# One shape of TensorE tile, 64 rows by 32 columns, for the attention to the context

## The chip, the cores and the metric

The kernel runs on one core of one Trainium2 chip. The core has a matrix engine (TensorE, called PE in the profile, with its weight loads as PEld), three engines for vectors (VectorE or DVE, ScalarE or ACT, GpSimd or POOL) and a queue for transfers (SyncE or SP). They run side by side and wait for each other through semaphores. The metric is the device time of one execution in microseconds, as a median of runs.

## The reference

It is one transformer block in 32-bit floats on x of 2 x 1024 x 256, with a context of 2 x 154 x 192: self-attention, attention to the context, and a gated feed-forward layer, each behind a layer norm and added to x. There are 16 heads of 64.

```python
def _attention(xq, xkv, wq, wk, wv, wo, bo):
    q = (xq @ wq).reshape(B, S, N_HEADS, D_HEAD)
    k = (xkv @ wk).reshape(B, T, N_HEADS, D_HEAD)
    v = (xkv @ wv).reshape(B, T, N_HEADS, D_HEAD)
    attn = jnp.einsum('bihd,bjhd->bhij', q, k) * scale
    attn = jax.nn.softmax(attn, axis=-1)
    out = jnp.einsum('bhij,bjhd->bihd', attn, v).reshape(B, S, D_ATTN)
    return out @ wo + bo

x = _attention(_layernorm(x), _layernorm(x), sa_...) + x
x = _attention(_layernorm(x), cond, ca_...) + x
p = _layernorm(x) @ ff_w1 + ff_b1
x = (p[:, :DF] * gelu(p[:, DF:])) @ ff_w2 + ff_b2 + x
```

## The kernel before

The array of TensorE, 128 rows by 128 columns, can be divided into tiles. A matmul uses the rows on whose partitions its operands lie and the columns on whose partitions its result lies: with 64 rows of operands and 32 partitions of result there are eight such tiles, with 64 by 64 four, with 64 by 128 two, with 128 by 128 one. [...]

The work goes in units: a unit is one sequence (of two) and one pair of heads (of eight), so sixteen units in each attention. A pair of heads fills 128 partitions, 64 each. The order of all instructions is written out by hand: one loop runs over the slots of self-attention, one over the 48 slots c of the attention to the context (three for each unit), one over the slots of the feed-forward layer. Each slot emits its pieces one after another, and each engine executes its own in that order.

In self-attention everything is in tiles of 64 by 32, apart from the values' projection: the projections of queries and keys (`project_both`, L352, with m = KB = 32), the scores (`scores`, L483) and the weighed values (`weigh`, L530).

A slot of the attention to the context holds these pieces:

- `cross_first` (L772) computes the scores of three tiles of 128 queries (two in every third slot), both heads, against the 154 keys of the context. Each matmul takes 64 rows (the head's dimension), 128 queries as its columns, and 154 keys as its moving operand. VectorE takes the maximum of each row, ScalarE the exponent, and a slot later VectorE and GpSimd divide by the sum.
- `cross_queries` (L352) projects the queries of the next unit, in every slot n = 0. Without an argument it uses m = P = 128 columns. Only the first unit's, which is emitted during self-attention through `cross_pieces`, is called with KB.
- `cross_drain` transposes the weights on VectorE, and `cross_regroup` moves them with eight transfers, so that two blocks of 32 keys lie together on 64 partitions.
- `cross_weigh` calls `cross_values` (L851) twice, which multiplies the weights by the values: 64 rows (keys), 64 columns (one head's dimension), 256 queries as the moving operand, three groups m of keys summed up in PSUM.
- Between them stand the output projections (L457), the values' projection of the context (L733), the keys of the context (L717), and the transposes of the layer norm (L270), which all take the whole array.

At the beginning of this stage the last pieces of self-attention (L530) are interleaved with its slots, at its end the first of the feed-forward layer (`gate_slot`, L933). The results of matmuls go to three pairs of PSUM banks: ps_s for scores and gates, ps_m and ps_o for the rest. A bank is used again when its reader has copied it out.

## Time and profile before

| | |
|---|---|
| time, median of 3 runs | 1115.72 us (1113.64 to 1117.36) |
| the profiled execution's own time | 1111.62 us |
| its span, from the first to the last instruction | 1109.7 us |
| instructions | 44860 |
| granted clock of TensorE | 1.00 |
| self-attention, with its preparation | up to about 722 us, the first scores of the context at 709.9 |
| attention to the context | from there to about 940 us |
| feed-forward layer | 918 us to the end |
| busy time of the scores, L772, in all | 41.6 us, 512 records |
| projected queries, L352, in 64 by 128 | 54.1 us, 240 records |
| weighed values, L851 | 35.2 us and 20.6 us, 768 records |

A line of a group or of the timeline names the line of the kernel, the operation, what it writes and reads, and for TensorE the tile of the array ("64*32") ahead of the moving operand ("64x512"). A matmul in 32-bit floats shows as two records, each with its weight load. Ends of matmuls are modelled, so the starts of what follows say more than durations. Busy time of a group is the time in which at least one of its records runs. In a table by stage each engine has its busy microseconds and, in brackets, its count.

### The profile page before, as it was taken

How to read it: one execution, taken by the hardware profiler on the slowest of the kernel's cores; microseconds unless marked ns; L12 is line 12 of the kernel's file. 1: busy time of each engine (PE TensorE's matmuls, PEld its weight loads, DVE VectorE, ACT ScalarE, POOL GpSimd, SP SyncE). 2: the span in 40 equal slices, each digit the busy share in tenths (PEclk: the TensorE clock that was granted, in tenths of full speed). 3: DMA queues.
4: the chain of work that ended last, by engine and by line, in shares of the span. 5: the costliest groups of instructions: out<-in, count | busy, mean ns of one | idle time of the engine just before them, and what ended most of it. 6: DMA issues, size and time to landing. Idle time of an engine off the chain costs nothing.

```text
span 1109.7 us, 44860 instructions
## 1 busy us (share of the span) xinstructions
PE 1093.7 (99%) x18436; PEld 733.5 (66%) x18436; DVE 855.1 (77%) x1205; ACT 628.2 (57%) x2030; POOL 681.4 (61%) x1584
## 2 busy tenths in 40 slices
PE   8999999999999999999999999999999999999998
PEld 6555656546556566666566565576766777888887
DVE  5889999898999899999999999868777875322222
ACT  4766666766666666667667666655556553121111
POOL 2777877777877787777777777756656653220000
PEclk9999999999999999999999999999999999999999
DMA  3222212111111012011111111136665443000000
GB/s 83 67 59 57 56 28 52 43 41 42 25 40 42 23 42 47 13 43 42 23 42 33 32 33 28 38 87 158 167 164 126 113 107 77 10 11 10 20 10 19
DMA packets 102350, 59.66 MB, mean 54 GB/s; under 512 B 31994, under 2 KB 92930, under 8 KB 102146
## 3 DMA queue, kind: packets, MB, share of 16 engines
q1 hardware_dynamic: 100914, 56.15, 21.3%
q8 instruction: 145, 2.38, 0.9%
q10 hardware_dynamic: 1232, 0.66, 0.2%
q14 instruction: 59, 0.48, 0.1%
HBM read 27.12 MB, written 2.10 MB: 26 GB/s over the span
## 4 chain that ended last, share of the span: by engine, by line
PE 56%; ACT 11%; DVE 10%; POOL 8%; DMA 7%; issue 4%; SPq 4%; DVEq 0%; POOLq 0%; ACTq 0%
PE pa L933 10%; ACT p L494 10%; PE po L530 8%; PE s L483 8%; DVE st L645 6%; DMA st<-st 6%; PE py_ca L457 5%; PE pf L956 5%; PE pq_ca L352 4%; PE poc L851 4%; SPq L504 3%; POOL p L595 3%; PE sc L772 3%; PE py_sa L457 2%; PE pk_sa L352 2%
## 5 line engine op out<-in xcount | busy, mean ns | idle before, releaser
L494 ACT ACTIVATE p<-s,st 128x512 f32<-128x512 f32 x512 | 344.9, 686 | 194.0 <-DVE st L645 186.0
L595 POOL TENSOR_SCALAR p<-p,rd,ee 128x512 f32<-128x512 f32 x512 | 385.7, 768 | 46.7 <-DVE rd L591 45.4
L645 DVE TENSOR_REDUCE st<-s 128x2 f32<-128x1024 f32 x256 | 300.9, 1216 | 20.3 <-PE s L483 7.1
L609 DVE STREAM_TRANSPOSE pT<-p 128x1024 f32<-128x1024 f32 x256 | 302.3, 1218 | 0.3 <-POOL p L595 0.3
L483 PE MATMUL s<-k_sa,q_sa 64*32 64x512 f32 x4096 | 262.1, 592 | 7.4 <-ACT p L494 6.5
L530 PE MATMUL po<-pT,v_sa 64*32 64x256 f32 x8192 | 239.5, 376 | 0.9 <-DVE pT L609 0.9
L530 PEld LDWEIGHTS po<-pT,v_sa 64*32 64x32 f32 x8192 | 177.9, 106 | 70.5 <-issue 22.0
L483 PEld LDWEIGHTS s<-k_sa,q_sa 64*32 64x32 f32 x4096 | 78.8, 106 | 115.2 <-ACT p L494 66.4
L799 POOL TENSOR_SCALAR p<-p,rden 128x154 f32<-128x154 f32 x256 | 96.8, 398 | 76.0 <-DVE rden L796 75.6
L788 ACT ACTIVATE p<-sc,neg 128x154 f32<-128x154 f32 x256 | 96.2, 405 | 83.1 <-DVE rden L796 78.0
L942 DVE SCALAR_TENSOR_TENSOR u<-pa,cols,gate 128x256 f32<-128x256 f32 x64 | 31.0, 484 | 123.1 <-ACT gate L939 123.1
L933 PE MATMUL pa<-hT_ln,wf 128*128 128x256 f32 x512 | 121.1, 380 | 0.2 <-ACT p L788 0.2
L939 ACT ACTIVATE gate<-pa,cols 128x256 f32<-128x256 f32 x64 | 30.3, 474 | 147.8 <-PE pa L933 146.1
L933 PEld LDWEIGHTS pa<-hT_ln,wf 128*128 128x128 f32 x512 | 96.7, 190 | 14.0 <-issue 0.8
L494 ACT ACTIVATION_READ_ACCUMULATOR p<-s,st 128x1 f32 x512 | 103.8, 203 | 0.0
L383 PEld LDWEIGHTS pv_sa<-sa_wv,hT_ln 64*128 64x128 f32 x1024 | 59.0, 188 | 14.6 <-issue 5.9
L956 PE MATMUL pf<-wf,u 128*128 128x256 f32 x256 | 64.7, 379 | 0.0
L518 POOL TENSOR_TENSOR zz<-ee,st 128x8 f32<-128x8 f32 x128 | 25.9, 202 | 61.5 <-ACT ee L516 61.5
L383 PE MATMUL pv_sa<-sa_wv,hT_ln 64*128 64x128 f32 x1024 | 62.4, 276 | 0.1
L457 PE MATMUL py_sa<-sa_wo,o_sa 128*128 128x256 f32 x256 | 59.7, 385 | 0.0
L457 PE MATMUL py_ca<-ca_wo,o_ca 128*128 128x256 f32 x256 | 59.7, 381 | 0.0
L457 PEld LDWEIGHTS py_sa<-sa_wo,o_sa 128*128 128x128 f32 x256 | 47.3, 190 | 17.9 <-ACT v_sa L392 8.4
(87 smaller groups left out, 1265.4 us busy)
## 6 DMA issues: line engine op xcount, KB each, us to landing
wf<-pT_ca SPq DMA_DIRECT2D x128, 128.0 KB, 2.4
st<-st SPq DMA_DIRECT2D x512, 1.0 KB, 1.8
v_sa<-v_sa SPq DMA_DIRECT2D x32, 256.0 KB, 3.5
sa_wq<-in_L_xattn_sa_wq_dram SPq DMA_DIRECT2D x32, 128.0 KB, 3.0
sa_wk<-in_L_xattn_sa_wk_dram SPq DMA_DIRECT2D x32, 128.0 KB, 3.0
sa_wv<-in_L_xattn_sa_wv_dram SPq DMA_DIRECT2D x32, 128.0 KB, 3.1
ca_wq<-in_L_xattn_ca_wq_dram SPq DMA_DIRECT2D x32, 128.0 KB, 3.3
wf<-in_L_xattn_ff_w_dram SPq DMA_DIRECT2D x12, 256.0 KB, 4.0
```

Of the source, the lines that this page charges most:

```text
L383: nc.tensor.matmul(pv[r][:, i * P:(i + 1) * P], lhsT=h[own, c, i * P:(i + 1) * P], rhs=wt[own, c, :], start=(c == 0), stop=(c == NH - 1), ...
L457: nc.tensor.matmul(py[:, e * D:(e + 1) * D], lhsT=o[:, i, (t + e) * P:(t + e + 1) * P], rhs=wo[kind][:, g * HP + i, :], start=(i == 0), st ...
L483: nc.tensor.matmul(sc[a4 * KB:(a4 + 1) * KB, j, :], lhsT=q[r, c:c + KB], rhs=k[r, h * HB:(h + 1) * HB], start=True, stop=True, tile_positi ...
L494: nc.scalar.activation(pr[:, j, :], sc[:, j, :], AF.Exp, bias=st[:, 0, 0, i, j:j + 1], accum_out=st[:, 0, 1, i, j:j + 1],)
L530: nc.tensor.matmul(po[a2][d:d + KB, :QH // 2], lhsT=v[r, t, e, d:d + KB], rhs=pT[r, d // DH * NK + n, :], start=(t == 0 and e == 0), stop= ...
L595: nc.gpsimd.tensor_scalar(pr[:, j, :], pr[:, j, :], rd[:, c:c + 1], ee[:, 0, c:c + 1], op0=ALU.mult, op1=ALU.mult,)
L609: nc.vector.transpose(halves[h][:, :, c:c + KB], groups.pop(0).rearrange("p j (n k) -> p (j n) k", k=KB))
L645: nc.vector.tensor_reduce(st[:, 0, 0, i, :], sc[i], AX.X, ALU.max, negate=True)
L788: nc.scalar.activation(pr_[:, j, i, :T], sc[:, j, i * T:(i + 1) * T], AF.Exp, bias=neg[:, j, i:i + 1], accum_out=den[:, j, i:i + 1],)
L799: nc.gpsimd.tensor_scalar(pr_[:, j, i, :T], pr_[:, j, i, :T], rden[:, j, i:i + 1], 1.0, op0=ALU.mult, op1=ALU.mult,)
L933: nc.tensor.matmul(pa[:, half, :TF * P], lhsT=w1[:, c, half * DF + f * P:half * DF + (f + 1) * P], rhs=h[:, c, t0 * P:(t0 + TF) * P], star ...
L956: nc.tensor.matmul(sums[blk][i][:, :D], lhsT=sums[blk, "u"][:, f, i * P:(i + 1) * P], rhs=w2[:, f, :], start=(f == 0), stop=(f == NF - 1),)
```

## The change

Three places get tiles of 64 rows by 32 columns. A score matmul of 128 queries is parted into four of 32 queries. The queries' projection is done with 32 columns at a time for all units, so the argument m falls away. A matmul of weighed values for one head's 64 dimensions is parted into two of 32. What is computed, the place of each result in PSUM and the order of the pieces remain.

```diff
-    def cross_queries(b, pr, m=P, bank=mm_tile):
+    def cross_queries(b, pr, bank=mm_tile):
         q = qk["ca", b, pr] = p2.tile([P, S], F32, tag="QT", name=f"q_ca{b}_{pr}")
         pq = [bank(f"pq_ca{b}_{pr}_{r}") for r in range(2)]
-        project_both(pq, wsl["ca", pr, "q"], hT["ca", b], m)
+        project_both(pq, wsl["ca", pr, "q"], hT["ca", b], KB)
         return lambda: take_both(q, pq, scale)
...
-        return [costing(2, lambda: cross_queries(b, pr, KB)), costing(1, lambda: context_values(b, pr))]
+        return [costing(2, lambda: cross_queries(b, pr)), costing(1, lambda: context_values(b, pr))]
...
         for i in range(nt):
             for j in range(2):
                 r = slice(j * DH, (j + 1) * DH)
-                nc.tensor.matmul(
-                    sc[:, j, i * T:(i + 1) * T], lhsT=q[r, (t0 + i) * P:(t0 + i + 1) * P],
-                    rhs=k[r, :], start=True, stop=True,
-                )
+                for f in range(0, P, KB):
+                    c0 = (t0 + i) * P + f
+                    nc.tensor.matmul(
+                        sc[f:f + KB, j, i * T:(i + 1) * T], lhsT=q[r, c0:c0 + KB],
+                        rhs=k[r, :], start=True, stop=True, tile_position=(j * DH, f),
+                    )
...
                 r = slice(r0, r0 + QG)
-                for j in range(2):
+                for d in range(0, 2 * DH, KB):
                     nc.tensor.matmul(
-                        po[a4][j * DH:(j + 1) * DH, :NT * KB],
-                        lhsT=v[r, m + a2 * (m == NM), v0 + j * DH:v0 + (j + 1) * DH],
-                        rhs=pTc["pairs"][r, a2, m, j] if m < NM else
-                        pTc["ring"][r, ui % 3, NB - 1, j, :],
+                        po[a4][d:d + KB, :NT * KB],
+                        lhsT=v[r, m + a2 * (m == NM), v0 + d:v0 + d + KB],
+                        rhs=pTc["pairs"][r, a2, m, d // DH] if m < NM else
+                        pTc["ring"][r, ui % 3, NB - 1, d // DH, :],
                         start=(m == 0), stop=(m == NM),
-                        tile_position=(r0, j * DH),
+                        tile_position=(r0, d),
                     )
```

## The prediction

> **What bounds the kernel now.** I read the page's busy shares first, then the busy times by stage, then the TensorE timeline of one repeating stretch in the stage that the change touches, and two stretches where the same kinds of work already meet without a change of tile shape.

> ```profile
> span 1109.7 us, 44860 instructions
> PE 1093.7 (99%) x18436; PEld 733.5 (66%) x18436; DVE 855.1 (77%) x1205; ACT 628.2 (57%) x2030; POOL 681.4 (61%) x1584
> ...
> 735.00:910.00 175.00, 174.75 (x1550) 124.39 (x1547) 135.07 (x301) 99.67 (x458) 105.07 (x289) 1.00 0.58 138
> ```

> The last line is the stage of attention to the context: TensorE is busy 174.75 of 175.00 us, VectorE 135, ScalarE 100, GpSimd 105, and the granted clock is 1.00. TensorE sets the time there, so every nanosecond that its queue loses or gains counts, unless a wait takes it. But a busy TensorE can hide gaps, since the ends of matmuls are modelled; I therefore go by starts. One repeating stretch (start, duration, tile shape, operands, records):

> ```profile
> 772.48 1.09 PE L851 MATMUL poc<-wf,v_ca 64*64 64x256 f32 x16
> ...
> 775.23 1.58 PE L772 MATMUL sc<-kT,q_ca 64*128 64x154 f32 x20
> 776.65 3.60 PE L352 MATMUL pq_ca<-hT_ln,ca_wq 64*128 64x512 f32 x16
> 780.08 0.95 PE L772 MATMUL sc<-kT,q_ca 64*128 64x154 f32 x12
> 780.96 0.66 PE L270 MATMUL ph_ln<-ident,xn_ln 128*128 128x128 f32 x4
> ```

> From start to start: 48 records of weighed values (poc) take 2.75 us, 20 of scores (sc) 1.42, 16 of projected queries (pq_ca) 3.43, 12 of scores 0.88; in all 8.48 us. A matmul of the program shows as two records. Records on different tiles start together, in rounds: pq_ca runs two tiles at a time, so its 16 records are 8 rounds.

> Now neighbours of one shape:

> ```profile
> 621.73 3.66 PE L530 MATMUL po<-pT,v_sa 64*32 64x256 f32 x128
> 625.19 1.92 PE L483 MATMUL s<-k_sa,q_sa 64*32 64x512 f32 x32
> 626.90 3.64 PE L352 MATMUL pq_sa<-hT_ln,sa_wq 64*32 64x512 f32 x64
> 630.34 1.92 PE L483 MATMUL s<-k_sa,q_sa 64*32 64x512 f32 x32
> ```

> The same projection in 64 rows by 32 columns (pq_sa) takes 3.44 us for 64 records: 8 rounds of eight tiles, 0.43 us each, against 3.43 us for pq_ca. The finer tile gains and loses nothing in the array. The po piece takes 3.46 us for 16 rounds, 0.216 us each. Where scores of another shape stand around it:

> ```profile
> 722.05 3.69 PE L530 MATMUL po<-pT,v_sa 64*32 64x256 f32 x128 [0.88 <-DVE pT L609]
> 725.67 1.06 PE L772 MATMUL sc<-kT,q_ca 64*128 64x154 f32 x12
> 726.65 3.68 PE L530 MATMUL po<-pT,v_sa 64*32 64x256 f32 x128
> 730.27 0.79 PE L772 MATMUL sc<-kT,q_ca 64*128 64x154 f32 x8
> 730.99 3.72 PE L457 MATMUL py_sa<-sa_wo,o_sa 128*128 128x256 f32 x16
> ```

> po now takes 3.62 us: 0.16 us go to coming from and leaving for another shape.

> [...] the page's loads of 32, 64 and 128 columns take 106, 133 and 187 ns, steps of 27 and 54 ns[...]. [...] this trace's single records on different tiles start 7 ns apart[...].

> **The price of a change of shape.** Three groups of scores give it, to the third digit from their single records: with a change before and after (from 725.67) 6 rounds take 0.986 us, with one before (from 775.23) 10 rounds take 1.412, with one after (from 780.08) 6 rounds take 0.882. So entering costs 0.104, leaving 0.098, a round 0.131. [...] 128 columns 0.104, 64 columns 0.054, 32 columns 0.027 (steps as above). Leaving has a constant 0.091 and the spread of the starts within the last round: 7 ns from tile to tile, 0.007 for two tiles, 0.02 for four, 0.05 for eight. Check: poc, 12 rounds of 0.2156 plus 0.054 plus 0.111, is 2.752 (seen: 2.75); po above, 3.45 plus 0.027 plus 0.141, is 3.618 (seen: 3.62).

> **The change part by part.** Nothing but TensorE's instructions changes; order, waits, transfers and the other engines' work stay. Scores go from 256 to 1024 matmuls, the projected queries of fifteen units from 120 to 480, the weighed values from 384 to 768: about 1500 more matmuls, which are some 3000 more matmul records and as many weight loads. Rounds stay as they are, for four times the pieces run four times as many at once.

> The repeating stretch becomes: poc 12 x 0.2156 + 0.027 (entry), no exit, 2.61; scores 10 x 0.131, no entry, 1.31; queries 3.43; scores 6 x 0.131 + 0.141 (exit from eight tiles), 0.925. Sum 8.28 against 8.48: 0.198 us less. It occurs eleven times between 745 and 900 us: 2.18. The stretch from 757 us, where the scores are parted by a transpose, gains 0.24; that at 905, which has no queries, 0.20. At 913 us scores, values and scores again stand between 128*128 pieces and gain 0.18 + 0.165 + 0.06 = 0.40. Between 722 and 739 us po twice gains 0.167, three groups of scores 0.20, 0.06 and 0.08, and one loses 0.04: 0.63. The last two value pieces (923 and 937 us) stand alone among 128*128 pieces: +0.00. Sum: 3.65 us.

> What doesn't arrive: up to 722 us another 0.34 would be saved, but TensorE then waits 0.88 us for the last transpose of self-attention, whose chain runs over small transfers, GpSimd and VectorE; I count nothing. At 917.93 us the gate's first matmul waits about 0.26 us for ScalarE's exponents of the scores issued at 913; only the scores' own 0.18 moves that wait's end, so 0.23 is taken back. The other waits of this stage (0.25 us at 754, 0.28 at 863, 0.5 at 871) are released by work that starts from TensorE pieces after which nothing is shortened, so they move along. A further 0.1 for single waits: 3.3 us less.

> The profiled execution took 1111.62 us, 1.9 us around its span of 1109.7. It becomes 1108.3. The median of the runs, 1115.72, lies 4.1 us higher; the same saving gives 1112.4.

> **The unknown: how fast instructions come.** A round of eight short scores needs eight weight loads and eight matmuls in 131 ns, 8.2 ns per instruction. No stretch of before is that dense: po needs 13.5 and is never late. Bounds: if instructions came no faster than po's 13.5 ns, with about 30 waiting in the queue, 160 of them would take (160 - 30) x 13.5 = 1.76 us instead of 1.31, and the 96 of the second group 0.89 instead of 0.79: 0.55 us lost per stretch against 0.20 gained, some 5 us over fourteen stretches; with an empty queue about 10. From 11.6 ns per instruction on, the loss exceeds the gain. On the other side, no cost. I take nothing to 0.1 us, for two signs: in the trace's records the sequencer handles two semaphore instructions 110 ns apart with nothing between, and 125 ns apart with eight matmul instructions between them, so some 2 ns each; and in po late weight loads follow each other at 16.7 ns, which with the matmuls between is 8.3 ns per instruction. Semaphore instructions also hold the sequencer (two at the queries: 0.22 us), but TensorE's queue in 64*32 runs some 24 instructions ahead, about 0.35 us of scores.

> **Rivals.** First, the gain is given back: if VectorE or ScalarE were close behind, the waits would grow by what TensorE saves. For it: VectorE 77% busy here, and the waits named. Against it: eleven stretches in a row repeat within 0.01 us when no wait falls in them. Half absorbed: 1.5 us less, 1114.2. Second, and slower: the instruction supply in the short scores, as priced, near 1120 (1117 to 1126), decided at 11.6 ns per instruction. Third, tiles of eight don't run together in scores[...]; and s and po show eight at a time. Its time would be that of the second.

> **How the numbers follow.** To the saved changes of shape in full I give 0.62; its own spread is 1110.5 to 1113.5, and about a sixth of it falls inside 0.3% (1112.4 is just at that bound, which is about what a measurement of this kernel can tell from no change). Absorbed: 0.23, nearly all within 0.3%. Slower supply: 0.15, of which 0.02 stays within. So faster 0.52, same 0.35, slower 0.13. The range 1109.8 to 1117.0 holds the first two cases, the runs' own scatter (1113.64 to 1117.36 before) and the mild end of the third.

> **What would show it.** After: scores directly following poc start about 2.61 us after its start, 80 score records take 1.31 us, queries 3.43 to 3.44, the closing 48 records 0.92, and a stretch 8.28. po at 722 takes 3.45. Wrong would be: rounds of scores longer than 0.14 us (supply), a TensorE wait that appears before poc or py (absorbed), or a stretch still at 8.48 with no gap anywhere[...].

## The result, and the profile after

The changed kernel takes 1118.09 us (median of 12 runs, 1116.21 to 1121.61) against 1114.76 us of the kernel before in the same session (12 runs, 1112.94 to 1117.36). The ratio is 1.0030, with a 95% interval of 1.0019 to 1.0041: slower by 3.3 us, where the prediction had 3.3 us less. A later repetition gave 1.0024 (1.0012 to 1.0037).

The page of the changed kernel first, its span and its busy shares, and from the table by stage the same 175 us of attention to the context (columns: stretch, its length, then TensorE, its weight loads, VectorE, ScalarE and GpSimd with their busy microseconds and counts, the granted clock, the share of the transfer engines, GB/s):

```profile
span 1119.8 us, 50908 instructions
PE 1098.3 (98%) x21460; PEld 737.6 (66%) x21460; DVE 854.7 (76%) x1205; ACT 629.8 (56%) x2030; POOL 684.8 (61%) x1584
...
735.00:910.00 175.00, 172.28 (x3925) 124.48 (x3909) 129.96 (x290) 97.86 (x450) 104.95 (x286) 0.99 0.59 140
```

There are 3024 more matmul records and as many weight loads. TensorE, which was idle for 0.25 us of these 175 us before, is now idle for 2.7. The profiled execution, at 1121.61 us, is the longest of the twelve. The first scores of the context start at 709.9 us before and at 714.2 now, though up to there the program is the same; so I compare from these first scores to the start of the last unit's weighed values: 227.47 us before, 233.28 after.

Where nothing interferes, the prediction's arithmetic is there. This is the timeline of TensorE for the repeating stretch (start, duration, operands, tile, moving operand, records):

```profile
776.69 1.09 PE L853 MATMUL poc<-wf,v_ca 64*32 64x256 f32 x32
...
779.30 1.55 PE L774 MATMUL sc<-kT,q_ca 64*32 64x154 f32 x80
780.61 3.67 PE L352 MATMUL pq_ca<-hT_ln,ca_wq 64*32 64x512 f32 x64
784.05 1.04 PE L774 MATMUL sc<-kT,q_ca 64*32 64x154 f32 x48
785.02 0.66 PE L270 MATMUL ph_ln<-ident,xn_ln 128*128 128x128 f32 x4
```

From start to start: 2.61, 1.31, 3.44, 0.97, in all 8.33 us. It was 8.48; 8.28 was forecast. This unit of three slots, from its poc to the next, is 12.37 us where it was 12.52; others are 11.98 for 12.13.

But sixteen units do not all look like that. The same view of the next unit, and the list of what TensorE waited for in the stage:

```profile
791.67 1.51 PE L774 MATMUL sc<-kT,q_ca 64*32 64x154 f32 x76
...
793.41 2.02 PE L352 MATMUL pq_ca<-hT_ln,ca_wq 64*32 64x512 f32 x21
797.67 3.67 PE L352 MATMUL pq_ca<-hT_ln,ca_wq 64*32 64x512 f32 x37 [2.25 <-issue]
```

```profile
PE pq_ca L352 <- issue: 2.2, 1, 2.2
```

In the middle of the projected queries TensorE stands still for 2.25 us, and the profile finds nothing that it waited for ("issue"): no semaphore, no operand. The table by stage around the stop:

```profile
788.00:795.30 7.30, 7.30 (x204) 5.04 (x203) 5.98 (x13) 2.48 (x14) 4.31 (x12) 1.00 0.96 223
795.30:797.70 2.40, 0.15 (x6) 0.02 (x4) 1.51 (x4) 2.00 (x11) 2.40 (x7) 1.00 0.94 215
797.70:801.90 4.20, 4.20 (x53) 2.00 (x57) 0.00 (x0) 0.34 (x2) 1.18 (x4) 0.60 0.84 225
801.90:806.00 4.10, 4.10 (x60) 3.54 (x51) 2.96 (x8) 2.81 (x11) 1.64 (x5) 0.99 0.07 13
```

Before the stop the transfer engines are busy for 96%. The line after it has a mean granted clock of 0.60; in the trace's own records of the clock it is 0.50 for 3.41 us, from 798.57 on, and a round of queries takes 0.85 us instead of 0.43. This unit took 19.59 us from poc to poc, against 14.34 before: 5.25 us lost in one place. Smaller losses, 0.3 to 1.1 us, lie in the units from 820, 835 and 888 us. Taking for each unit from the second to the sixteenth the shorter one of the changed kernel's two profiles (a second one follows below), or 0.15 below the kernel before for the three that neither shows undisturbed, the sum is 190.3 us, 1.75 less than the 192.06 of before; they took 197.78. So the saving is real, about 1.75 us in these units, and 7.5 us are lost again in this execution.

What TensorE lacked is seen in the packets of queue q8, the larger of two that the page calls "instruction". Each brings 16384 bytes. The page has 145 such packets before and 169 after; TensorE's matmuls, weight loads and semaphore instructions are 257 to a packet in both, so I take a packet for a block of 256 of them. Between 735 and 940 us the packets are 15 and 36. Their times around the stop (start, duration, us), from the trace's records of single packets:

```
before     773.82 1.26   788.04 1.15   801.04 1.35
after      781.18 1.04   785.41 0.98   794.65 1.46   801.25 1.08
```

In this stage of the kernel before a block of 256 lasts 13 to 15 us, and a fetch of 1.3 us doesn't matter. In the changed kernel one lasts 2.8 to 4.5 us in the dense pieces, from its first instruction, with which TensorE enters it, to its last, with which it is used up (where blocks begin is seen from the stops further down). The fetch that began at 794.65 was preceded by 432 instructions since the last fetch, not 256: TensorE had used up what it had, and went on 1.56 us after the block had landed.

The theory to be tested, called T in the expectations: the time saved at changes of shape is as computed, and the loss comes from TensorE running out of fetched instructions, because the finer tiles need up to three times as many per microsecond. Its rivals: R1, the finer tiles cost more in the array or other waits take the saving; R2, the loss is chance.

### The profile page after: what moved, and what is told of

Same layout as the page of the kernel before. It is cut to its first block, busy times and chain, and to the rows that moved or that the text cites. A ratio compares the mean times of both kernels' runs of the same rounds, so it can differ in the third digit from the quotient of the medians.

```text
span 1119.8 us, 50908 instructions
## 1 busy us (share of the span) xinstructions
PE 1098.3 (98%) x21460; PEld 737.6 (66%) x21460; DVE 854.7 (76%) x1205; ACT 629.8 (56%) x2030; POOL 684.8 (61%) x1584
## 4 chain that ended last, share of the span: by engine, by line
PE 51%; ACT 13%; DVE 9%; DMA 9%; POOL 8%; issue 5%; SPq 4%; DVEq 0%; POOLq 0%; ACTq 0%
ACT p L494 11%; PE pa L935 10%; DMA st<-st 8%; PE s L483 6%; DVE st L645 6%; PE po L530 6%; PE pf L958 5%; PE py_ca L457 5%; SPq L504 4%; PE poc L853 4%; PE pq_ca L352 4%; POOL p L595 3%; PE py_sa L457 3%; PE sc L774 2%; PE pv_sa L383 2%
## 5 line engine op out<-in xcount | busy, mean ns | idle before, releaser
L609 DVE STREAM_TRANSPOSE pT<-p 128x1024 f32<-128x1024 f32 x256 | 302.3, 1218 | 0.3 <-POOL p L595 0.3
L483 PE MATMUL s<-k_sa,q_sa 64*32 64x512 f32 x4096 | 263.2, 593 | 8.5 <-ACT p L494 7.2
L530 PE MATMUL po<-pT,v_sa 64*32 64x256 f32 x8192 | 239.5, 376 | 1.1 <-DVE pT L609 1.0
L530 PEld LDWEIGHTS po<-pT,v_sa 64*32 64x32 f32 x8192 | 175.6, 106 | 73.1 <-issue 21.1
L483 PEld LDWEIGHTS s<-k_sa,q_sa 64*32 64x32 f32 x4096 | 77.7, 106 | 118.7 <-ACT p L494 74.4
L352 PE MATMUL pq_ca<-hT_ln,ca_wq 64*32 64x512 f32 x1024 | 64.1, 602 | 2.4 <-issue 2.2
L779 DVE TENSOR_REDUCE neg<-sc 128x6 f32<-128x924 f32 (+1 forms) x48 | 47.7, 996 | 17.8 <-PE sc L774 17.6
L457 PE MATMUL py_sa<-sa_wo,o_sa 128*128 128x256 f32 x256 | 59.7, 385 | 0.0
```

Source lines behind the costliest of these rows:

```text
L352: nc.tensor.matmul(pq[r][f:f + m, at:at + n], lhsT=wt[own, c, f:f + m], rhs=h[own, c, t0:t0 + n], start=(c == 0), stop=(c == NH - 1), tile ...
L457: nc.tensor.matmul(py[:, e * D:(e + 1) * D], lhsT=o[:, i, (t + e) * P:(t + e + 1) * P], rhs=wo[kind][:, g * HP + i, :], start=(i == 0), st ...
L483: nc.tensor.matmul(sc[a4 * KB:(a4 + 1) * KB, j, :], lhsT=q[r, c:c + KB], rhs=k[r, h * HB:(h + 1) * HB], start=True, stop=True, tile_positi ...
L530: nc.tensor.matmul(po[a2][d:d + KB, :QH // 2], lhsT=v[r, t, e, d:d + KB], rhs=pT[r, d // DH * NK + n, :], start=(t == 0 and e == 0), stop= ...
L609: nc.vector.transpose(halves[h][:, :, c:c + KB], groups.pop(0).rearrange("p j (n k) -> p (j n) k", k=KB))
```

## The experiments

**The changed kernel once more.**

> The changed kernel once more, for a second profile. Theory T: again about 3 us slower than before, again stops of TensorE for which no wait is shown, longest where transfers are busy between 785 and 900 us, though not of the same length and at the same place. Rival R2 (chance): the loss against before is gone or of the other sign, and no such stops.

1118.32 us (10 runs), ratio 1.0024 (1.0012 to 1.0037). Its second profile, TensorE's timeline at the same unit:

```profile
793.45 1.01 PE L352 MATMUL pq_ca<-hT_ln,ca_wq 64*32 64x512 f32 x2
795.11 1.91 PE L352 MATMUL pq_ca<-hT_ln,ca_wq 64*32 64x512 f32 x20 [0.65 <-DMA ca_wq<-in_L_xattn_ca_wq_dram]
797.59 2.36 PE L352 MATMUL pq_ca<-hT_ln,ca_wq 64*32 64x512 f32 x37 [0.57 <-issue]
```

The stop recurs at the same place, after 22 of 64 records, and the fetch that ends it again comes late: it begins 9.4 us after the one before it (785.42, then 794.79), in the first profile 9.2. The clock stays at 1.00 this time, and the unit takes 17.62 us. Ahead of it there is a second wait: the weights ca_wq, loaded by a transfer, are 0.65 us late. R2 is out. The second profile has the loss of this unit without the clock: about 3.4 us (17.62 less 14.19) for late instructions and weights. In the first it is about 2 us more, of which I estimate 1.7, half of the 3.41 us, for the clock.

**The same saving with fewer instructions.** Four tiles of 64 by 64 instead of eight of 64 by 32.

```diff
-    def cross_queries(b, pr, m=P, bank=mm_tile):
+    def cross_queries(b, pr, m=DH, bank=mm_tile):
...
-                nc.tensor.matmul(
-                    sc[:, j, i * T:(i + 1) * T], lhsT=q[r, (t0 + i) * P:(t0 + i + 1) * P],
-                    rhs=k[r, :], start=True, stop=True,
-                )
+                for f in range(0, P, DH):
+                    c0 = (t0 + i) * P + f
+                    nc.tensor.matmul(
+                        sc[f:f + DH, j, i * T:(i + 1) * T], lhsT=q[r, c0:c0 + DH],
+                        rhs=k[r, :], start=True, stop=True, tile_position=(j * DH, f),
+                    )
```

> The kernel before, with the context's scores in two pieces of 64 queries and the queries' projection in 64 columns; the weighed values stay at 64 by 64. So poc, scores and queries again have one shape[...], but a unit of the repeating stretch gets about 96 more TensorE instructions instead of 384. Theory T ([...]the loss comes from instructions that run out): 2 to 2.5 us faster than before, about 1112.5, a repeating stretch 0.2 us shorter, no stop of TensorE inside the queries' projection. Rival R1 ([...]other waits take the saving): within 0.5 us of before, or slower. Rival R2 (the loss of the changed kernel is chance): no prediction.

1113.08 us (22 runs), ratio 0.9981 (0.9973 to 0.9989): 2.1 us faster. The stretch, on TensorE's timeline:

```profile
775.63 1.09 PE L853 MATMUL poc<-wf,v_ca 64*64 64x256 f32 x16
...
778.27 1.49 PE L774 MATMUL sc<-kT,q_ca 64*64 64x154 f32 x40
779.58 3.61 PE L352 MATMUL pq_ca<-hT_ln,ca_wq 64*64 64x512 f32 x32
783.01 0.96 PE L774 MATMUL sc<-kT,q_ca 64*64 64x154 f32 x24
783.91 0.66 PE L270 MATMUL ph_ln<-ident,xn_ln 128*128 128x128 f32 x4
```

2.64, 1.31, 3.43, 0.90, in all 8.28 us: 0.20 less than before. In this stage the list of waits has no "issue". From the first scores to the last weighed values the kernel takes 225.34 us, 2.13 less than before, which is the whole gain of the medians. Theory T's forecast came in; R1 would have had no gain. A stretch has 288 TensorE instructions here (96 + 80 + 64 + 48), where the kernel before has 192 and the changed one 576 (192 + 160 + 128 + 96).

**Fewer transfers beside it.** In both kernels the regrouping transfers are left out for fifteen of the sixteen units, so that the first unit's blocks are read again.

```diff
-        if n != 0 or not 0 <= ui < NU:
+        if n != 0 or ui != 0:
```

> The changed kernel, which leaves out the regrouping transfers of the weights for fifteen of the sixteen units (the blocks of the first unit are read again in their place). To be compared with the same omission in the kernel before. Theory T: with fewer transfers in the way the instruction fetches come in time, so this runs 2 to 3.5 us faster than the kernel before with the same omission, and TensorE does not stop inside the queries' projection. Rival R1 (finer tiles cost more in the array, whatever the transfers): some 3 us slower than the kernel before with the same omission.

> The kernel before, which leaves out the regrouping transfers of the weights for fifteen of the sixteen units. Both theories: within 1 us of before, since TensorE does not wait for these transfers in the repeating stretches; it is the base for the changed kernel with the same omission.

With the change 1114.23 us, ratio to before 0.9999 (0.9990 to 1.0008); without it 1114.68 us, 0.9998 (0.9987 to 1.0009). So the loss of 3.3 us is gone, but the gain of 2 to 3.5 us that T named has not come: both theories miss, R1 by more. At the unit of the stop the timeline has

```profile
791.40 3.68 PE L352 MATMUL pq_ca<-hT_ln,ca_wq 64*32 64x512 f32 x61
```

without a stop, and the fetches begin at 785.57, 789.99 and 793.76. The middle one is that which was missing: it came 2.6 us after the start of poc, where in the changed kernel the same place is 791.65, and the fetch began at 794.65, 3.0 us late. In those 3 us the regrouping transfers were being issued and the transfer engines were full; whether issuing or moving holds the fetch up isn't shown, since the omission takes away both. Units 2 to 16 take 191.45 us against 192.07 of the kernel before with the same omission, so of the 1.75 us some 1.1 is still lost, in pieces too small for the list of waits.

**More instructions in the old tiles.** The shapes stay; the moving operand of the queries is parted into four, that of the weighed values into two.

```diff
-        project_both(pq, wsl["ca", pr, "q"], hT["ca", b], m)
+        project_both(pq, wsl["ca", pr, "q"], hT["ca", b], m, step=P if m == P else None)
...
-        for m in range(NM + 1):
+        for o in range(0, NT * KB, P):
+          for m in range(NM + 1):
...
-                        po[a4][j * DH:(j + 1) * DH, :NT * KB],
+                        po[a4][j * DH:(j + 1) * DH, o:o + P],
```

> The kernel before with its tile shapes, but the moving operand of the projected queries parted into four of 128 columns and that of the weighed values into two of 128: the same tiles, as many changes of shape, and about 192 more TensorE instructions in a unit. The parts themselves cost an estimated 0.085 us in a unit, 1.3 us in all. Theory T: 2.5 to 5 us slower than before, with stops of TensorE (no wait shown) inside these pieces, as in the changed kernel. Rival R1: 1.3 us slower, and no stops.

1116.86 us, ratio 1.0013 (1.0005 to 1.0022), 1.7 us slower, and in this stage no stop with "issue" on TensorE. The stretch:

```profile
778.76 0.67 PE L856 MATMUL poc<-wf,v_ca 64*64 64x128 f32 x16
...
781.54 1.58 PE L774 MATMUL sc<-kT,q_ca 64*128 64x154 f32 x20
782.95 3.74 PE L354 MATMUL pq_ca<-hT_ln,ca_wq 64*128 64x128 f32 x64
786.52 0.95 PE L774 MATMUL sc<-kT,q_ca 64*128 64x154 f32 x12
787.41 0.66 PE L270 MATMUL ph_ln<-ident,xn_ln 128*128 128x128 f32 x4
```

Most units are longer by the same 0.17 us (12.69 for 12.52, 12.30 for 12.13), twice the 0.085 estimated (36 more rounds of some 2.4 ns each: in the trace of before two rounds of 256 columns, 0.2157 us each, last 2.4 ns more than one of 512, 0.4290). So T missed here: 384 instructions in a stretch of 8.65 us do not exhaust the supply. That is 256 in 5.8 us on average, and no block of this stage is used up in less than 5.0; the changed kernel's 576 in 8.33 us are 256 in 3.7, and its densest block is used up in 2.8. What decides is how soon a block is used up, not how many instructions there are in all. The next pair of runs looks at that by itself.

**The supply measured: every score matmul four times.** The same edit in both kernels, a loop around the score matmuls, which write the same result again.

```diff
+        for _ in range(4):
             for i in range(nt):
                 for j in range(2):
```

> The changed kernel with every score matmul of the attention to the context done four times over (same result, written again). At 8.2 ns per TensorE instruction, 48 more rounds of 0.131 us in a unit are 6.29 us, in sixteen units 100.6 us. Theory T (TensorE runs out of fetched instructions in dense stretches): the repeated scores use 256 instructions in 2.1 us, sooner than a block can be fetched, so they run at the rate of the fetches, some 3.5 to 4 us for each 256, and this kernel ends 40 to 100 us later than its counterpart in 64 by 128. Rival R1 (the finer tile as such): within 5 us of the counterpart.

> The kernel before with every score matmul of the attention to the context done four times over, in its tiles of 64 by 128. A round of 0.131 us has two matmuls of the program here, so instructions come at 33 ns. Both theories: 100 us longer than before, near 1216, and the repeated rounds 0.131 us each.

In 64 by 128 1212.97 us, in 64 by 32 1291.15 us (two runs each): 78 us apart for the same arithmetic in the array. First the 64 by 128 kernel's timeline, then that of the 64 by 32 kernel, then TensorE's waits of the latter:

```profile
765.09 5.50 PE L773 MATMUL sc<-kT,q_ca 64*128 64x154 f32 x80
770.43 3.60 PE L352 MATMUL pq_ca<-hT_ln,ca_wq 64*128 64x512 f32 x16
```

```profile
834.15 2.32 PE L775 MATMUL sc<-kT,q_ca 64*32 64x154 f32 x127
836.88 2.33 PE L775 MATMUL sc<-kT,q_ca 64*32 64x154 f32 x128 [0.41 <-issue]
840.63 1.36 PE L775 MATMUL sc<-kT,q_ca 64*32 64x154 f32 x65 [1.42 <-issue]
841.70 4.32 PE L352 MATMUL pq_ca<-hT_ln,ca_wq 64*32 64x512 f32 x63
```

```profile
PE sc L775 <- issue: 47.8, 38, 3.0
```

Eighty records, 40 rounds, take 5.34 us in 64 by 128, 0.133 us each with one entry: no stop. The same 40 rounds in 64 by 32, 320 records, take 7.55 us (834.15 to 841.70). TensorE does 128 matmul records, which with their 128 weight loads are 256 instructions, at full pace in 2.3 us, and stops; then again 128, and stops. The third block, 65 records of scores and 63 of queries, ends in a stop too. From one TensorE record's start to the next there are 46 stops of over 0.6 us in this stage (three more gaps are rounds at half the clock), and between any two of them lies a whole multiple of 256 instructions. The stops of the changed kernel stand on the same grid: counted from the program's start, 35265 instructions precede the long one and 39617 that in the unit from 888 us, in both profiles, and both numbers leave the remainder 193 when divided by 256. So do the numbers of all 46. This shows the cause: TensorE waits for blocks of instructions.

The packets show how long a block takes: in this stretch they begin at 834.49 and 838.00 and last 1.14 and 1.29 us, and TensorE goes on at 836.88 and 840.63. Over these stops: the fetch lasts 1.07 us (median), TensorE goes on 1.36 us after it has landed (1.11 to 1.62), and the next fetch begins 1.05 us after that at the earliest. That is a circle of some 3.5 us, in which nothing overlaps, or 13.7 ns for each of 256 instructions. The closest starts of two fetches are 3.3 us apart, half of them over 4.0. In all thirteen traces a fetch begins at the earliest 2.3 us after the one before has landed. A single block can be used up sooner without a stop, if it came early: one of 2.8 us in the changed kernel did so. And the pace itself brings no stop: in self-attention of the kernel before nine blocks are used up in 3.30 to 3.66 us, one of them in the po piece at 621.73 that the prediction shows (128 records, 256 instructions, 3.46 us), and there TensorE has no wait with "issue".

**How much of it the transfers do.** The scores four times, and the regrouping left out for fifteen units as above.

> The changed kernel with every score matmul done four times, which leaves out the regrouping transfers of fifteen of the sixteen units. Is the rate of fetches set by itself or by the transfers beside it? In the same kernel with the transfers, fetches in the dense stretches begin 3.3 to 5 us apart. If the transfers hold the fetches up: the intervals gather at 3.5 us and the time falls by 15 to 30 us from 1291. If a fetch has its own pace: the same as 1291 within 5 us.

1285.02 us (two runs, 1281.17 and 1288.87), 6 us less than 1291.15: just outside the 5 us named for a pace of its own, and far from the 15 to 30 us named for the transfers. The fetches in the stage have a median distance of 3.87 us instead of 4.04, and a tenth of them are under 3.53 in both. So the transfers beside it account for some 6 of 78 us, with two runs on each side: most of the pace is the fetch's own. In the changed kernel they matter more, since there the margin is small. Of its blocks in this stage eleven are used up in 2.8 to 4.1 us. The fetch of the next one begins 0.86 us (median) after such a block is entered, against 0.51 without the regrouping and 0.44 in self-attention of the kernel before, where the transfer engines are busy for 16% and not 59%. With the 1.07 and 1.36 us from above, a block needs an estimated 3.3, 2.9 and 2.9 us to be ready. So some of the densest blocks of the first profile end in stops of up to 0.6 us, and the fetch that began 3.8 us after the block before it had been entered makes the stop of 2.25 us.

That late fetch isn't peculiar to the changed kernel. At the same place it begins 4.2 us after the block before it was entered in the kernel with 64 by 64 (at 792.51 us), and 4.2 us in the one with the scores alone in 64 by 32 (at 791.15 us). The first uses up its block in 7.4 us and doesn't stop; the second does so in 5.7 us and stops for 0.7. That the late weights in the second profile have the same origin is plausible, but wasn't tried.

**The prices of a change of shape.** Part of the change alone, so that a change of shape stands between all the pieces: the changed kernel with the scores in 64 by 128, and the kernel before with only the scores in 64 by 32 (the diff of the change's score part, removed and added).

> The changed kernel with the scores in 64 by 128 again, queries and weighed values in 64 by 32. The scores now stand alone in their shape: by the prices of a change of shape, leaving poc 0.03 dearer and entering it 0.027 cheaper than before, leaving the scores 0.098, entering the queries 0.027, leaving them 0.141, entering the scores 0.104, in all 0.37 us more than before in a repeating stretch, some 5 us in all. Theory T: that, and hardly a stop of TensorE, for the densest instructions are gone: 5 us slower than before. Rival R1 (queries or weighed values in 64 by 32 cost more in themselves): over 7 us slower.

> The kernel before with the scores alone in 64 by 32. By the prices of a change of shape, a repeating stretch has 0.336 us more than before, some 4.7 us in all. The scores' instructions come at 8.2 ns for 160 at a time, less than one fetched block of 256. Theory T: 5 us slower than before, with few stops, less than 1 us in all. Rival R1 (the scores in 64 by 32 cost more in themselves): over 7 us slower, in the score rounds.

1119.93 us, ratio 1.0036 (1.0023 to 1.0050), and 1120.06 us, 1.0036 (1.0026 to 1.0047), both 4.1 to 4.3 us slower; units are 0.36 us longer in the first (12.49 for 12.13) and 0.34 in the second (12.47), forecast 0.37 and 0.336. The first kernel's timeline, then the second's:

```profile
847.09 1.09 PE L851 MATMUL poc<-wf,v_ca 64*32 64x256 f32 x32
...
849.84 1.58 PE L772 MATMUL sc<-kT,q_ca 64*128 64x154 f32 x20
851.35 3.66 PE L352 MATMUL pq_ca<-hT_ln,ca_wq 64*32 64x512 f32 x64
854.94 1.06 PE L772 MATMUL sc<-kT,q_ca 64*128 64x154 f32 x12
```

```profile
843.58 1.09 PE L853 MATMUL poc<-wf,v_ca 64*64 64x256 f32 x16
...
846.34 1.55 PE L774 MATMUL sc<-kT,q_ca 64*32 64x154 f32 x80
847.81 3.70 PE L352 MATMUL pq_ca<-hT_ln,ca_wq 64*128 64x512 f32 x16
851.45 1.03 PE L774 MATMUL sc<-kT,q_ca 64*32 64x154 f32 x48
```

From start to start 2.75, 1.51, 3.59 and 2.76, 1.47, 3.64. By the prediction's prices the first are 2.587 + 0.027 + 0.141 = 2.755, 0.104 + 1.31 + 0.098 = 1.512, 0.027 + 3.43 + 0.141 = 3.598, the second 2.752, 0.027 + 1.31 + 0.141 = 1.478, 0.104 + 3.43 + 0.098 = 3.632. The prices hold to 0.01 us. Against T's "less than 1 us in all", the second has one stop of 0.7 us, in the unit from 789 us, which is 1.2 us longer than its like.

**Fine tiles only at the beginning.** 64 by 32 for the scores and queries that stand beside self-attention's pieces of that shape, 64 by 64 afterwards.

```diff
+                step = KB if c < 2 * len(CG) else DH
+                for f in range(0, P, step):
...
-                run(lambda: cross_queries(*nxt))
+                run(lambda: cross_queries(*nxt, KB))
```

> Tiles of 64 by 32 for the scores of the first six slots and the queries of the first three units, where they stand beside self-attention's pieces of that shape; 64 by 64 for everything of the attention to the context after that, as in the kernel with 64 by 64 throughout. Theory T: 2.1 to 2.7 us faster than before, about 1112.5, no stop of TensorE. Rival R1: no more than 0.5 us faster.

1113.60 us, ratio 0.9987 (0.9976 to 0.9999), 1.7 us faster by the medians, not better than 64 by 64 throughout (1113.08); T's 2.1 to 2.7 was too much. Units 2 to 16 take 189.72 us, as in 64 by 64 (189.75). The first unit has 36.39 us for 35.58 and holds a stop of 0.3 us with "issue" in po. That stop stands on the grid of 256 as well, but part of this difference is scatter in the wait for self-attention's last transposes (35.41 before, 34.52 without the regrouping), and how much wasn't settled.

## Why the prediction was wrong

**What bounds the kernel, and the price of a change of shape: right.** TensorE sets the time, entering and leaving a shape cost what was read from three groups of scores, and the runs that add such changes come out as priced. The entry into 64 and 32 columns, 0.054 and 0.027 us, was an estimate from the steps of 54 and 27 ns in the weight loads' times. In the trace of before the first round behind a change lasts 0.267 us for 0.216 in 64 by 64 (poc at 772.48), 0.240 for 0.216 in 64 by 32 (po at 726.65) and 0.235 for 0.131 in 64 by 128 (scores at 775.23): 0.051, 0.024 and 0.104 more. What the array does at a change wasn't shown, only its time.

**The change part by part: right in size where TensorE has its instructions.** Of the falsifiers, scores follow poc after 2.61 us as forecast, 80 score records take 1.31, queries 3.44. The closing group was mis-sized: 0.97 instead of 0.92, so a stretch is 8.33 and not 8.28, and saves 0.15 and not 0.198. The same exit came out as priced in the kernel with the scores alone in 64 by 32; why it is dearer behind the queries is open. Between 722 and 739 us po took 3.45 as forecast once, and 3.79 the second time, with a stop. That the gate's wait gives part back came as expected: the unit in which it lies is 9.80 us for 9.55.

**The step that failed: "The unknown: how fast instructions come", with "I take nothing to 0.1 us".** Its question was how fast the sequencer hands out instructions that it has, and there the answer was right: rounds of eight short scores run at 0.131 us, 8.2 ns per instruction. Both signs that I drew on, the semaphores 110 and 125 ns apart and the weight loads 16.7 ns apart, are of that kind, short bursts inside a block. The instructions must also come in by transfer, in blocks of 256 (one packet of 16384 bytes each), and where TensorE stops for them a block takes 3.5 us. Part of this was at hand: the packets of the instruction queue in the trace of the kernel before, one every 13 to 15 us in this stage and each of 0.9 to 1.35 us, showed that a fetch is no matter of nanoseconds. Self-attention in the same trace would even have spoken for the prediction, since blocks used up in 3.30 to 3.66 us pass there without a stop; what it didn't show is a denser block, or one beside so many transfers. The break-even of 11.6 ns per instruction was set for the scores alone. The mean of the whole stretch, 14.5 ns, is above the 13.7 ns of the fetches and gives no warning either. What had to be compared is the densest block: the 96 instructions of half the poc and the 160 of the scores behind it are 256 in 2.6 us by the forecast itself, less than the 2.9 to 3.3 us that the runs showed a block to need.

The falsifier of that rival looked in the wrong place, too: "rounds of scores longer than 0.14 us". The rounds stay at 0.131; the long stop comes a piece later, in the queries, whose own instructions are few.

**The rivals.** The second, slower supply, 0.15, was the one that came: its range of 1117 to 1126 holds 1118.09, and its subject was right, its mechanism not. That the number fits is luck: it was worked out from scores that run slowly throughout, and they didn't. (Its bound for an empty queue, "about 10", comes to some 16 by the sum that it gives: 2.16 for 1.31 and 1.30 for 0.79 us, less 0.20, fourteen times. The 24 instructions by which it has the queue ahead are 0.20 us of scores at 8.2 ns each, and not 0.35.) The first, absorbed savings, did not occur beyond the gate's wait. That tiles of eight run together in scores, the third's question, is shown by the 80 records in 1.31 us.

**The sum.** Forecast -3.3, measured +3.3. In the second profile units 2 to 16 take 196.92 for 192.06 us: 1.75 saved and 6.6 lost in stops and in waits for transfers, 3.4 of it in the one unit from 789 us. Both profiled executions (1121.61 and 1120.40 us) are longer than the medians of their runs, so these 4.9 us are more than a median execution can have lost; how the 3.3 us divide isn't on record.

## What to carry to other kernels

When an edit cuts matmuls into more and smaller ones, look for the 256 instructions of the engine that are used up soonest, not only at the time in the array. In this kernel blocks that last over 6 us passed without a stop, one of them with a fetch that began 4.2 us after the block was entered; blocks of 3.3 to 3.7 us passed where the transfer engines were busy for 16%; where they were busy for 59%, blocks of 2.8 to 5.7 us ended in stops now and then; and where one block of 2.0 us followed another, each took some 3.5 to 4 us. Take the coarsest tile that gives all neighbours one shape: 64 by 64 had the saving of 64 by 32 with half the instructions, and is 2.1 us faster than the kernel before. All 46 stops of over 0.6 us in the 64 by 32 kernel with its scores four times lie whole multiples of 256 instructions apart, and so do the changed kernel's two (35265 and 39617 instructions from the start): in these traces a stop marked "issue" on that grid was a wait for instructions.

## What the runs showed of the hardware that I had not expected

The granted clock fell after some of the long stops. Over the profiles of the changed kernel and of its two variants with the scores four times, ten stops lasted 2.26 to 3.33 us from one record's start to the next (the one shown, with 2.25 us idle, is 2.84 by this measure). Seven of them were followed by a granted clock of 0.50 for 3.41 us, an estimated loss of 1.7 us each; of the stops of up to 2.0 us none was. Within a trace these falls begin whole multiples of 3.413 us from one another (40.96 and 238.93 us in one, 23.89 and 98.99 in the other). On that grid the ten sort themselves: the seven had 2.2 us or more of the stop within one interval of 3.41 us, the three had 2.1 at most. That is a sorting of ten cases, and not a threshold for waits of other kinds: waits of 0.76 and 1.73 us within one interval, at 723 us in the second profile of the changed kernel, were not followed by a fall. Here is the table by stage of the kernel with the scores four times, before and after its longest stop:

```profile
764.00:767.00 3.00, 0.54 (x34) 0.23 (x16) 0.00 (x0) 0.00 (x0) 0.00 (x0) 1.00 0.98 256
767.00:771.00 4.00, 3.42 (x48) 1.25 (x56) 2.55 (x5) 1.31 (x7) 1.24 (x4) 0.57 0.11 23
771.00:775.00 4.00, 4.00 (x176) 2.73 (x168) 0.77 (x4) 2.14 (x8) 1.04 (x3) 1.00 0.01 4
```

So of ten stops of 2.3 to 3.3 us on instructions seven cost an estimated 1.7 us more (half of the 3.41 us at a clock of 0.50). Two stops of 2.26 us differ in this: one was followed by a fall and one was not, the first with 2.2 us or more of it within one interval of 3.413 us, the second with 2.1 at most. Every one of the ten was shorter than an interval of that grid, 3.33 us at most.
